# A two-layer cross-attention kernel: the transposed operands split by half of the tokens, the work between the layers and the last linear layer put in another order

## The chip, the cores and the metric

The kernel runs on one core of a Trainium2 chip. The metric is device time in microseconds (us); the time of the kernel before is the median of three runs. A profiled execution gives the trace that the prediction is worked out from.

## The reference, cut to what matters

1024 tokens (16 sequences of 64) of width 512 pass four residual blocks, all in fp32:

```
x += L0_attention(layernorm(x), ctx)   # 32 query heads, 8 key/value heads of 128, rope, tanh cap, masked softmax
x += L0_experts(layernorm(x))          # 4 low-rank experts of rank 16, the best 2 by router logits
x += L1_attention(layernorm(x), ctx)   # 16 query heads, 4 key/value heads of 96, keys from [ctx, x]
x += L1_linear(layernorm(x))           # x W^T + bias + 16 low-rank updates, merged into W
```

## The kernel before, in words

The tokens lie in eight tiles of 128 rows, `xt[0..7]`; tiles 0 to 3 are half 0, tiles 4 to 7 are half 1. The matmuls need tokens along the free dimension, so one tile `hT` (128 x 2 x 4 x 1024) holds the transposed context (index 0, loaded by DMA) and the transposed normalised x (index 1). `ln_stats` (L183) takes the statistics of a half on VectorE (DVE): `bn_stats` (L188) and `bn_aggr` (L189) per tile, then the square root on ScalarE (ACT, L191) and a reciprocal (L192). `normed[i]` is `ln_tile(i)` (L196): DVE scales the tile into `xn` (L199), TensorE (PE) makes four transposes into PSUM (`tp`, L202), ACT copies them into `hT` (L203). This happens four times for each tile: at the start, between the layers ahead of the experts and again ahead of layer 1's attention, and ahead of the last linear layer.

Buffers: PSUM has four tags of two buffers each. `pa` holds projections, `tp` and `mp`; `pb` holds scores, softmax sums and small transposes; `pc` holds the attention product; `pd` holds what is added into x. `xn` and the last layer's output `ot` share a tag of two buffers in SBUF.

The attention of a layer is cut into items. In layer 0 an item (kv, half, quad) has four steps: `l0_scores` (PE L317, tanh and exp on ACT, two masking passes on POOL, L331 and L334), `l0_norm` (PE sum L342, the DVE reciprocal `r` of 128x512, L344, POOL product L346), `l0_av` (PE L358, four ACT copies L367) and `l0_wo` (16 matmuls L379, DVE add into x L386). In layer 1 an item (kv, half, pair) has `l1_scores` (PE L577, DVE maximum L585, exp L590, POOL product L599), `l1_transpose` (L605), `l1_av` (L615, copies L623 and L627) and `l1_wo` (L635).

The order is written out by hand in slots. Each item takes 4 slots (`SLOTS`), its steps lie at fixed distances (`LAGS`), and `BETWEEN` slots separate the layers. Everything else (projections, norms, experts, linear layer) is a filler put into a slot. `_run` goes through the slots and emits a slot's steps first, then its fillers. PE takes its instructions in exactly this order (`manual_schedule` for PE alone); the orders of DVE, ACT and POOL are made by the tile framework. So PE waits wherever its next instruction is not ready.

h0 is the slot in which layer 0's last step on half 0 falls, 116; h1, for half 1, is 132; layer 1 begins at slot u0 = 136. The order around h0, half 0's change of layers (steps | fillers):

```
116 wo(7,0,1) scores(6,1,1) | q_chunk 3, ln_stats        122 av(6,1,1)               | experts gT + 4 outputs
117                         | normed 0, 1                123 norm(7,1,0)             | ln_stats
118 av(6,1,0)               | normed 2, 3                124 wo(6,1,1) scores(7,1,1) | normed 0, 1
119 norm(6,1,1)             | experts_mid                125                         | normed 2, 3
120 wo(6,1,0) scores(7,1,0) |                            126 av(7,1,0)               | v_chunk 0, 1 of layer 1
```

Half 1 follows at h1 in the same manner, spread among layer 1's projections and first items. `experts_mid` (L430) multiplies with the experts and the router (`mp`, L434), then a chain of some 18 small DVE operations with one exp on ACT makes the gated product `gm` (L475). `experts_out` (L483) transposes it (`gtp`, L487), copies it (`gT`, L489), and makes one output matmul per tile (`pm`, L494; even tiles use rows 0 to 63, odd ones rows 64 to 127), which DVE adds into x (L495).

At the end, `linear(i)` (L676) adds the bias to x on POOL (L677), multiplies `hT` with the merged weight (`pf`, 8 matmuls, L680), adds on DVE into `ot` (L688) and stores it from SyncE's queue (L689). Its order after the projections have run out, with the last items of layer 1 (unit (3,1), pairs p0 to p3):

```
258 linear 0 | 259 wo p0 | 260 av p1, scores p3 | 261 transpose p2 | 262 linear 1 | 263 wo p1
264 av p2, stats 4 5 | 265 transpose p3 | 266 normed 4, linear 2 | 267 wo p2, stats 6, normed 5
268 av p3 | 269 linear 3 | 270 normed 6 | 271 wo p3, stats 7, linear 4, 5, normed 7, linear 6, 7
```

Of the kernel before, what the change touches and what calls it, by code (L numbers as in the profile page):

```python
# [72 lines left out]
LAGS = ((0, 3, 6, 8), (0, 5, 8, 11))  # L73


BETWEEN = 8
AHEAD = 2


# [8 lines left out]
def two_layer_kernel(  # L88
# [33 lines left out]

    hT = const.tile([P, 2, KC, NTOK], F32, tag="hT", name="hT")
    xt = [const.tile([P, D], F32, tag=f"x{i}", name=f"x{i}") for i in range(NT)]
    cos_sb = const.tile([P, S], F32, tag="cos", name="cos_sb")
    sin_sb = const.tile([P, S], F32, tag="sin", name="sin_sb")
# [5 lines left out]
    def load_ctx(half):  # L134
        for c in range(KC):
            nc.sync.dma_start(
                out=hT[:, 0, c, ts(half, HALF)], in_=ctxT[ts(c, P), ts(half, HALF)]
            )

    def load_x(half):  # L140
# [55 lines left out]
    def ln_tile(i):  # L196
        mean, rstd = ln[i]
        xn = work.tile([P, D], F32, tag="xn", name="xn")
        nc.vector.tensor_scalar(xn, xt[i], mean, rstd, ALU.subtract, ALU.mult)  # L199
        tp = ps.tile([P, KC, P], F32, tag="pa", name="tp")  # L200
        for c in range(KC):
            nc.tensor.transpose(tp[:, c, :], xn[:, ts(c, P)], ident)  # L202
        nc.scalar.copy(hT[:, 1, :, ts(i, P)], tp)  # L203

    halves = [range(0, NT // 2), range(NT // 2, NT)]

# [33 lines left out]
    v0 = {}  # L240

    def l0_unit(kv, half):
        tok = ds(half * HALF, HALF)
        unit = {"kv": kv, "half": half}

        def rope(pr, dst):
            cos_b = cos_sb.unsqueeze(1).to_broadcast([P, HALF // S, S])
            sin_b = sin_sb.unsqueeze(1).to_broadcast([P, HALF // S, S])
            sh = work.tile([P, HALF], F32, tag="sh", name="sh")
            nc.scalar.copy(sh[0:64, :], pr[64:128, :])  # L250
            nc.scalar.copy(sh[64:128, :], pr[0:64, :])  # L251
            u = work.tile([P, HALF], F32, tag="u", name="u")
            nc.vector.tensor_tensor(  # L253
                u.rearrange("p (b t) -> p b t", t=S),
                pr.rearrange("p (b t) -> p b t", t=S),
                cos_b,
                ALU.mult,
            )
            w = work.tile([P, HALF], F32, tag="w", name="w")
            nc.gpsimd.tensor_tensor(  # L260
                w.rearrange("p (b t) -> p b t", t=S),
                sh.rearrange("p (b t) -> p b t", t=S),
                sin_b,
                ALU.mult,
            )
            nc.vector.tensor_tensor(dst, u, w, ALU.add)  # L266

        def k_chunk():
            unit["k"] = act.tile([P, HALF], F32, tag="k", name="kT")
            unit["q"] = act.tile([P, G0, HALF], F32, tag="q", name="qT")  # L270
            pr = ps.tile([P, HALF], F32, tag="pa", name="pk")
            for c in range(KC):
                nc.tensor.matmul(  # L273
                    pr, lhsT=w0[kv][1][:, c, :], rhs=hT[:, 0, c, tok], start=c == 0, stop=c == KC - 1
                )
            rope(pr, unit["k"])

        def q_chunk(g):
            pr = ps.tile([P, HALF], F32, tag="pa", name="pq")
            for c in range(KC):  # L280
                nc.tensor.matmul(  # L281
                    pr,
                    lhsT=w0[kv][0][:, c, ts(g, HD0)],
                    rhs=hT[:, 1, c, tok],
                    start=c == 0,
                    stop=c == KC - 1,
                )
            rope(pr, unit["q"][:, g, :])

        def v_chunk(n):  # L290
            if n == 0:
                v0[kv // 2] = act.tile([P, NT, 2 * HD0], F32, tag="v", name="v")
            pr = ps.tile([P, 2, 2 * HD0], F32, tag="pa", name="pv")
            for i in range(2):
                for c in range(KC):
                    nc.tensor.matmul(  # L296
                        pr[:, i, :],
                        lhsT=hT[:, 0, c, ts(2 * n + i, P)],
                        rhs=w0[kv][2][:, c, :],
                        start=c == 0,  # L300
                        stop=c == KC - 1,
                    )
            nc.scalar.copy(v0[kv // 2][:, 2 * n : 2 * n + 2, :], pr)

        context = [k_chunk]
        if half == 0 and kv % 2 == 0:
            context += [lambda n=n: v_chunk(n) for n in range(4)]
        queries = [lambda g=g: q_chunk(g) for g in range(G0)]
        return context, queries, [{"unit": unit, "quad": qd} for qd in range(2)]

# [119 lines left out]
    def experts_mid(grp):  # L430
        mp = ps.tile([P, 4, NM + NE], F32, tag="pa", name="mp")
        for n in range(4):
            for c in range(KC):
                nc.tensor.matmul(  # L434
                    mp[:, n, :],
                    lhsT=hT[:, 1, c, ts(grp * 4 + n, P)],
                    rhs=aw[:, c, :],
                    start=c == 0,
                    stop=c == KC - 1,
                )  # L440
# [39 lines left out]
        )  # L480
        experts[grp] = gm

    def experts_out(grp):  # L483
        gmf = experts[grp].rearrange("p n e r -> p (n e r)")
        tp = ps.tile([P, 2, P], F32, tag="pb", name="gtp")
        for m in range(2):
            nc.tensor.transpose(tp[:, m, :], gmf[:, ts(m, P)], ident)  # L487
        gT = work.tile([P, 2, P], F32, tag="gT", name="gT")
        nc.scalar.copy(gT, tp)  # L489
        for n in range(4):  # L490
            i = grp * 4 + n
            rows = slice((n % 2) * NM, (n % 2 + 1) * NM)
            po = ps.tile([P, D], F32, tag="pd", name="pm")
            nc.tensor.matmul(po, lhsT=gT[rows, n // 2, :], rhs=bcat[rows, :], start=True, stop=True)  # L494
            nc.vector.tensor_add(xt[i], po, xt[i])  # L495


# [4 lines left out]
    def l1_unit(kv, half):  # L502
# [1 line left out]
        nb = B // 2  # L504

        def k_chunk(n):
            tok = ds(half * HALF + n * 256, 256)
            pr = ps.tile([P, 2, 256], F32, tag="pa", name="pk1")
            for c in range(KC):
                nc.tensor.matmul(  # L510
                    pr,
                    lhsT=w1s[kv][1][:, c, :],
                    rhs=hT[:, :, c, tok],
                    start=c == 0,
                    stop=c == KC - 1,
                )
            prb = pr.rearrange("d s (b t) -> d b s t", t=S)
            nc.scalar.copy(unit["k"][:, n * 4 : n * 4 + 4], prb[0:HD1])
            b0 = half * nb + n * 4
            nc.scalar.copy(k_last[ts(kv, TH), b0 : b0 + 4], prb[HD1:P])  # L520
# [10 lines left out]
        def q_chunk(g):  # L531
            pr = ps.tile([P, HALF], F32, tag="pa", name="pq1")
            for c in range(KC):
                nc.tensor.matmul(  # L534
                    pr,
                    lhsT=w1s[kv][0][:, c, ts(g, P)],
                    rhs=hT[:, 1, c, ds(half * HALF, HALF)],
                    start=c == 0,
                    stop=c == KC - 1,
                )  # L540
# [4 lines left out]
        def v_chunk(b):  # L545
# [2 lines left out]
                v1[half] = act.tile([P, nb, KV1 * HD1], F32, tag="v", name="v1")  # L548
            hv = work.tile([P, KC, 2, S], F32, tag="sh", name="hv")
            for s in range(2):  # L550
                nc.gpsimd.tensor_copy(hv[:, :, s, :], hT[:, s, :, ts(b, S)])
            pr = ps.tile([P, KV1 * HD1], F32, tag="pa", name="pv1")
            for c in range(KC):
                nc.tensor.matmul(  # L554
# [121 lines left out]
    def linear(i):  # L676
        nc.gpsimd.tensor_tensor(xt[i], xt[i], bias_bc, ALU.add)  # L677
        po = ps.tile([P, D], F32, tag="pd", name="pf")
        for c in range(KC):
            nc.tensor.matmul(  # L680
                po,
                lhsT=hT[:, 1, c, ts(i, P)],
                rhs=lin["w"][:, c, :],
                start=c == 0,
                stop=c == KC - 1,
            )
# [85 lines left out]
    put(begin[0, (6, 1)] + 13, lambda: load_wo1(0))  # L772
    put(begin[0, (7, 1)] + 13, lambda: load_wo1(1))
    for half, t in ((0, h0), (1, h1)):
        at = (1, 3, 6, 7, 8) if half == 0 else (2, 4, 8, 9, 11)
        mine = [normed[i] for i in halves[half]]
        put(t, lambda half=half: ln_stats(*halves[half]))
        put(t + at[0], *mine[:2])
        put(t + at[0] + 1, *mine[2:])
        put(t + at[1], lambda half=half: experts_mid(half))  # L780
        put(t + at[2], lambda half=half: experts_out(half))
        put(t + at[3], lambda half=half: ln_stats(*halves[half]))
        put(t + at[4], *mine[:2])
        put(t + at[4] + 1, *mine[2:])
    spread(h0 + 10, u0 - 1, built1[0, 0][0])
    spread(u0 - AHEAD, begin[1, (1, 0)] - AHEAD, built1[1, 0][0])
    spread(h1 + 13, u1 - AHEAD, built1[0, 1][0])
    for a, b in zip(units1[2:], units1[3:]):
        spread(begin[1, a] - AHEAD, begin[1, b] - AHEAD, built1[b][0])
    for kv in (2, 3):  # L790
# [17 lines left out]
    def applied(i):  # L808
        return lambda: linear(i)

    put(last + 10, applied(0))
    put(last + 14, applied(1))
    put(last + 16, stats(4, 5))
    put(last + 18, normed[4], applied(2))
    put(last + 19, stats(6), normed[5])
    put(last + 21, applied(3))
    put(last + 22, normed[6])
    put(h1, stats(7), applied(4), applied(5), normed[7], applied(6), applied(7))
    _run(stages, fillers)


# [42 lines left out]
```

## Time and profile before

| | |
|---|---|
| median of three runs | 1091.32 us (1090.82 to 1091.77) |
| the profiled execution's own time | 1091.71 us |
| its span, first to last instruction | 1089.8 us |
| its mean granted PE clock | 0.994 |
| busy: PE, DVE, ACT, POOL | 96%, 40%, 30%, 27% of the span |
| DMA | 38.56 MB, mean 35 GB/s |

The table comes from the page's head and its first parts. A busy PE is counted with modelled ends of matmuls; the chain of waits shows how many microseconds a run of matmuls holds PE, and the windows show where it stood idle or had a lower clock.

### The profile page before, as it was taken

How to read it: one execution, taken by the hardware profiler on the slowest of the kernel's cores; microseconds unless marked ns; L12 is line 12 of the kernel's file. 1: busy time of each engine (PE TensorE's matmuls, PEld its weight loads, DVE VectorE, ACT ScalarE, POOL GpSimd, SP SyncE). 2: the span in 40 equal slices, each digit the busy share in tenths (PEclk: the TensorE clock that was granted, in tenths of full speed). 3: DMA queues.
4: the chain of work that ended last, by engine and by line, in shares of the span. 5: the costliest groups of instructions: out<-in, count | busy, mean ns of one | idle time of the engine just before them, and what ended most of it. 6: DMA issues, size and time to landing. Idle time of an engine off the chain costs nothing.

```text
span 1089.8 us, 9319 instructions
## 1 busy us (share of the span) xinstructions
PE 1051.7 (96%) x3398; PEld 532.3 (49%) x3398; DVE 436.3 (40%) x641; ACT 327.3 (30%) x844; POOL 291.8 (27%) x263
## 2 busy tenths in 40 slices
PE   7789999999999999999999999998999999999987
PEld 5334455444455444446444444545565555555643
DVE  3345342435432434432434555314322334435532
ACT  2342232232232232231322241224333343334420
POOL 2143332433331433331433331200121011112210
PEclk9999999999999999999999998999999999999999
DMA  9310020010020010020010100110001000110001
GB/s 320 102 39 0 11 78 19 10 53 25 11 78 14 10 46 31 11 78 15 1 38 10 39 30 0 29 29 1 1 22 39 18 30 29 29 39 1 1 29 49
DMA packets 26157, 38.56 MB, mean 35 GB/s; under 512 B 1824, under 2 KB 12064, under 8 KB 26112
## 3 DMA queue, kind: packets, MB, share of 16 engines
q1 hardware_dynamic: 25840, 37.63, 10.5%
q8 instruction: 27, 0.44, 0.2%
q0 software_dynamic: 272, 0.34, 0.2%
q14 instruction: 18, 0.15, 0.0%
HBM read 35.87 MB, written 2.10 MB: 35 GB/s over the span
## 4 chain that ended last, share of the span: by engine, by line
PE 93%; ACT 3%; DVE 2%; DMA 1%; POOL 1%; issue 0%; SPq 0%; DVEq 0%; ACTq 0%
PE pq L281 20%; PE po L379 20%; PE pq L534 8%; PE po L635 8%; PE pk L273 6%; PE pv L296 4%; PE pk L510 4%; PE pv L554 4%; PE sc L317 3%; PE av L358 3%; PE pf L680 3%; PE sm L342 3%; PE av L615 2%; PE sc L577 2%; PE tp L605 1%; PE tp L202 1%
## 5 line engine op out<-in xcount | busy, mean ns | idle before, releaser
L281 PE MATMUL pq<-hT,wq 128*128 128x512 f32 x512 | 234.3, 602 | 6.6 <-ACT hT L203 6.6
L379 PE MATMUL po<-wo,at 128*128 128x512 f32 x512 | 225.9, 594 | 0.0
L260 POOL TENSOR_TENSOR w<-sh,sin_sb 128x512 f32<-128x512 f32 x80 | 106.7, 1333 | 197.7 <-ACT sh L251 197.2
L379 PEld LDWEIGHTS po<-wo,at 128*128 128x128 f32 x512 | 97.8, 191 | 121.4 <-issue 120.2
L281 PEld LDWEIGHTS pq<-hT,wq 128*128 128x128 f32 x512 | 93.7, 190 | 123.2 <-issue 110.1
L344 DVE RECIPROCAL r<-sm 128x512 f32<-128x512 f32 x32 | 107.4, 3357 | 107.6 <-PE sm L342 107.6
L253 DVE TENSOR_TENSOR u<-pq,cos_sb 128x512 f32<-128x512 f32 x64 | 43.1, 673 | 142.7 <-ACT sh L251 142.7
L599 POOL TENSOR_TENSOR e<-e,sm 128x512 f32<-128x512 f32 x32 | 33.3, 1039 | 244.5 <-DVE sm L598 237.3
L635 PE MATMUL po<-wo_sb,at 128*128 128x512 f32 x192 | 87.8, 593 | 0.1
L250 ACT COPY sh<-pq 64x512 f32<-64x512 f32 x64 | 37.3, 582 | 166.9 <-PE pq L281 166.9
L534 PE MATMUL pq<-hT,wq_sb 128*128 128x512 f32 x192 | 86.5, 595 | 0.6 <-ACT hT L203 0.6
L331 POOL TENSOR_TENSOR e<-e,keep 128x512 f32<-128x512 f32 x32 | 40.5, 1266 | 170.0 <-ACT e L330 170.0
L386 DVE TENSOR_TENSOR x<-po,x 128x512 f32<-128x512 f32 x64 | 44.0, 687 | 99.9 <-PE po L379 99.9
L326 ACT ACTIVATE e<-sc 128x512 f32<-128x512 f32 x32 | 19.1, 597 | 204.4 <-PE sc L317 204.3
L273 PE MATMUL pk<-hT,wk 128*128 128x512 f32 x128 | 63.2, 637 | 5.2 <-DMA hT<-in_ctxT 5.0
L266 DVE TENSOR_TENSOR qT<-u,w 128x512 f32<-128x512 f32 x64 | 49.3, 771 | 31.8 <-POOL w L260 31.3
L346 POOL TENSOR_TENSOR en<-e,r 128x512 f32<-128x512 f32 x32 | 41.0, 1282 | 76.6 <-DVE r L344 76.6
L296 PE MATMUL pv<-wv,hT 128*128 128x256 f32 x256 | 57.6, 381 | 1.2 <-DMA wv<-in_wv 0.8
L635 PEld LDWEIGHTS po<-wo_sb,at 128*128 128x128 f32 x192 | 35.8, 190 | 41.3 <-issue 35.3
L534 PEld LDWEIGHTS pq<-hT,wq_sb 128*128 128x128 f32 x192 | 35.1, 190 | 39.7 <-issue 37.1
L296 PEld LDWEIGHTS pv<-wv,hT 128*128 128x128 f32 x256 | 48.3, 190 | 12.3 <-issue 4.0
L642 DVE TENSOR_TENSOR x<-po,x 128x512 f32<-128x512 f32 x32 | 22.1, 690 | 75.3 <-PE po L635 75.2
(111 smaller groups left out, 1130.1 us busy)
## 6 DMA issues: line engine op xcount, KB each, us to landing
wq<-in_wq SPq DMA_DIRECT2D x8, 1024.0 KB, 5.7
wo<-in_wo SPq DMA_DIRECT2D x8, 1024.0 KB, 5.1
wq_sb<-in_wq SPq DMA_DIRECT2D x4, 768.0 KB, 4.7
wo_sb<-in_wo SPq DMA_DIRECT2D x4, 768.0 KB, 4.6
wk<-in_wk SPq DMA_DIRECT2D x8, 256.0 KB, 2.7
hT<-in_ctxT SPq DMA_DIRECT2D x8, 256.0 KB, 5.5
wv<-in_wv SPq DMA_DIRECT2D x4, 512.0 KB, 5.4
x<-in_x SPq DMA_DIRECT2D x8, 256.0 KB, 7.2
```

Source lines behind the costliest of these rows:

```text
L260: nc.gpsimd.tensor_tensor(w.rearrange("p (b t) -> p b t", t=S), sh.rearrange("p (b t) -> p b t", t=S), sin_b, ALU.mult,)
L266: nc.vector.tensor_tensor(dst, u, w, ALU.add)
L273: nc.tensor.matmul(pr, lhsT=w0[kv][1][:, c, :], rhs=hT[:, 0, c, tok], start=c == 0, stop=c == KC - 1)
L281: nc.tensor.matmul(pr, lhsT=w0[kv][0][:, c, ts(g, HD0)], rhs=hT[:, 1, c, tok], start=c == 0, stop=c == KC - 1,)
L296: nc.tensor.matmul(pr[:, i, :], lhsT=hT[:, 0, c, ts(2 * n + i, P)], rhs=w0[kv][2][:, c, :], start=c == 0, stop=c == KC - 1,)
L344: nc.vector.reciprocal(r, sm)
L379: nc.tensor.matmul(po, lhsT=it["at"][:, g, ts(pr, P)], rhs=wo[:, g, :], start=g == 0, stop=g == G0 - 1,)
L386: nc.vector.tensor_add(xt[i], po, xt[i])
L510: nc.tensor.matmul(pr, lhsT=w1s[kv][1][:, c, :], rhs=hT[:, :, c, tok], start=c == 0, stop=c == KC - 1,)
L534: nc.tensor.matmul(pr, lhsT=w1s[kv][0][:, c, ts(g, P)], rhs=hT[:, 1, c, ds(half * HALF, HALF)], start=c == 0, stop=c == KC - 1,)
L554: nc.tensor.matmul(pr, lhsT=hv[:, c].rearrange("p s t -> p (s t)"), rhs=wv1s[c // 2][:, c % 2, :], start=c == 0, stop=c == KC - 1,)
L635: nc.tensor.matmul(po, lhsT=it["at"][:, g].rearrange("d m t -> d (m t)"), rhs=w1s[u["kv"]][2][:, g, :], start=g == 0, stop=g == PK1 - 1,)
```

## The change

`hT` becomes two tiles, one per half (`hT[h]`, 128 x 2 x 4 x 512), and each use names its half. `experts_out` is cut in two: `experts_gT` (transposes and copy) and `experts_out(grp, pair)` (two of the four outputs), in slots of their own. `BETWEEN` goes from 8 to 10, so layer 1 begins at slot 138. Between the layers and in the last linear layer the fillers get other slots:

```diff
-BETWEEN = 8
+BETWEEN = 10
...
-    hT = const.tile([P, 2, KC, NTOK], F32, tag="hT", name="hT")
+    hT = [const.tile([P, 2, KC, HALF], F32, tag=f"hT{h}", name=f"hT{h}") for h in range(2)]
...
-        nc.scalar.copy(hT[:, 1, :, ts(i, P)], tp)
+        nc.scalar.copy(hT[i // 4][:, 1, :, ts(i % 4, P)], tp)
...
-    def experts_out(grp):
+    def experts_gT(grp):
...
         nc.scalar.copy(gT, tp)
-        for n in range(4):
+        experts[grp] = gT
+
+    def experts_out(grp, pair):
+        for n in (2 * pair, 2 * pair + 1):
...
-        at = (1, 3, 6, 7, 8) if half == 0 else (2, 4, 8, 9, 11)
+        norm1, mid, gates, out0, norm2 = (2, 4, 7, 8, 11) if half == 0 else (3, 5, 9, 10, 14)
...
+        put(t + norm1, a, b)
+        put(t + norm1 + 1, c, d)
+        put(t + mid, lambda half=half: experts_mid(half))
+        put(t + gates, lambda half=half: experts_gT(half))
+        put(t + out0, lambda half=half: experts_out(half, 0))
+        put(t + out0 + 1, lambda half=half: experts_out(half, 1), lambda half=half: ln_stats(*halves[half]))
+        put(t + norm2, a, b)
+        put(t + norm2 + 1, c, d)
-    spread(h0 + 10, u0 - 1, built1[0, 0][0])
+    spread(h0 + 13, u0, built1[0, 0][0])
...
-    spread(h1 + 13, u1 - AHEAD, built1[0, 1][0])
+    spread(h1 + 16, u1 - AHEAD, built1[0, 1][0])
...
-    put(last + 10, applied(0))
-    put(last + 14, applied(1))
-    put(last + 16, stats(4, 5))
-    put(last + 18, normed[4], applied(2))
-    put(last + 19, stats(6), normed[5])
-    put(last + 21, applied(3))
-    put(last + 22, normed[6])
-    put(h1, stats(7), applied(4), applied(5), normed[7], applied(6), applied(7))
+    put(last + 15, stats(4, 5))
+    put(last + 18, applied(0))
+    put(last + 19, normed[4], stats(6))
+    put(last + 20, normed[5])
+    put(last + 22, applied(1))
+    put(h1, stats(7), applied(2), normed[6], applied(3), applied(4), applied(5))
+    put(h1 + 1, normed[7], applied(6), applied(7))
```

The same three places in the new order, worked out from the code. Around h0 (slot 116 unchanged but for what follows it):

```
117                         |                            123 norm(7,1,0)             | gT
118 av(6,1,0)               | normed 0, 1                124 wo(6,1,1) scores(7,1,1) | outputs 0, 1
119 norm(6,1,1)             | normed 2, 3                125                         | outputs 2, 3, ln_stats
120 wo(6,1,0) scores(7,1,0) | experts_mid                126 av(7,1,0)               |
121                         |                            127 norm(7,1,1)             | normed 0, 1
122 av(6,1,1)               |                            128 wo(7,1,0)               | normed 2, 3
```

Around h1: `normed 4, 5` follow layer 1's first k projection, `normed 6, 7` the first q projection; `experts_mid` and the last q projection stand directly ahead of layer 1's first `l1_scores` (138); gT comes at 141, outputs 4, 5 at 142, outputs 6, 7 and `ln_stats` at 143; then a q projection (145), av p0, scores p2, `normed 4, 5` (146), transpose p1, `normed 6, 7` (147). At the end: scores p3, transpose p2, wo p1, stats 4 5, av p2, transpose p3, linear 0, wo p2, normed 4, stats 6, av p3, normed 5, linear 1, wo p3, stats 7, linear 2, normed 6, linear 3, 4, 5, normed 7, linear 6, 7.

More of the change, by code (lines that the diff above doesn't have):

```diff
@@ L136, in load_ctx @@
             nc.sync.dma_start(
-                out=hT[:, 0, c, ts(half, HALF)], in_=ctxT[ts(c, P), ts(half, HALF)]
+                out=hT[half][:, 0, c, :], in_=ctxT[ts(c, P), ts(half, HALF)]
             )
@@ L242, in l0_unit @@
     def l0_unit(kv, half):
-        tok = ds(half * HALF, HALF)
         unit = {"kv": kv, "half": half}
@@ L273, in k_chunk @@
                 nc.tensor.matmul(
-                    pr, lhsT=w0[kv][1][:, c, :], rhs=hT[:, 0, c, tok], start=c == 0, stop=c == KC - 1
+                    pr, lhsT=w0[kv][1][:, c, :], rhs=hT[half][:, 0, c, :], start=c == 0, stop=c == KC - 1
                 )
@@ L283, in q_chunk @@
                     lhsT=w0[kv][0][:, c, ts(g, HD0)],
-                    rhs=hT[:, 1, c, tok],
+                    rhs=hT[half][:, 1, c, :],
                     start=c == 0,
@@ L297, in v_chunk @@
                         pr[:, i, :],
-                        lhsT=hT[:, 0, c, ts(2 * n + i, P)],
+                        lhsT=hT[n // 2][:, 0, c, ts(2 * (n % 2) + i, P)],
                         rhs=w0[kv][2][:, c, :],
@@ L435, in experts_mid @@
                     mp[:, n, :],
-                    lhsT=hT[:, 1, c, ts(grp * 4 + n, P)],
+                    lhsT=hT[grp][:, 1, c, ts(n, P)],
                     rhs=aw[:, c, :],
@@ L493, in experts_out @@
             po = ps.tile([P, D], F32, tag="pd", name="pm")
-            nc.tensor.matmul(po, lhsT=gT[rows, n // 2, :], rhs=bcat[rows, :], start=True, stop=True)
+            nc.tensor.matmul(
+                po, lhsT=experts[grp][rows, n // 2, :], rhs=bcat[rows, :], start=True, stop=True
+            )
             nc.vector.tensor_add(xt[i], po, xt[i])
@@ L506, in k_chunk @@
         def k_chunk(n):
-            tok = ds(half * HALF + n * 256, 256)
             pr = ps.tile([P, 2, 256], F32, tag="pa", name="pk1")
@@ L512, in k_chunk @@
                     lhsT=w1s[kv][1][:, c, :],
-                    rhs=hT[:, :, c, tok],
+                    rhs=hT[half][:, :, c, ds(n * 256, 256)],
                     start=c == 0,
@@ L536, in q_chunk @@
                     lhsT=w1s[kv][0][:, c, ts(g, P)],
-                    rhs=hT[:, 1, c, ds(half * HALF, HALF)],
+                    rhs=hT[half][:, 1, c, :],
                     start=c == 0,
@@ L550, in v_chunk @@
             for s in range(2):
-                nc.gpsimd.tensor_copy(hv[:, :, s, :], hT[:, s, :, ts(b, S)])
+                nc.gpsimd.tensor_copy(hv[:, :, s, :], hT[half][:, s, :, ts(b % nb, S)])
             pr = ps.tile([P, KV1 * HD1], F32, tag="pa", name="pv1")
@@ L681, in linear @@
                 po,
-                lhsT=hT[:, 1, c, ts(i, P)],
+                lhsT=hT[i // 4][:, 1, c, ts(i % 4, P)],
                 rhs=lin["w"][:, c, :],
@@ L774, in two_layer_kernel @@
     for half, t in ((0, h0), (1, h1)):
-        at = (1, 3, 6, 7, 8) if half == 0 else (2, 4, 8, 9, 11)
-        mine = [normed[i] for i in halves[half]]
+        norm1, mid, gates, out0, norm2 = (2, 4, 7, 8, 11) if half == 0 else (3, 5, 9, 10, 14)
+        a, b, c, d = [normed[i] for i in halves[half]]
         put(t, lambda half=half: ln_stats(*halves[half]))
[L778 to L784, printed above, removed]
-    spread(h0 + 10, u0 - 1, built1[0, 0][0])
+        put(t + norm1, a, b)
[7 more added lines that the diff above has]
+    spread(h0 + 13, u0, built1[0, 0][0])
     spread(u0 - AHEAD, begin[1, (1, 0)] - AHEAD, built1[1, 0][0])
-    spread(h1 + 13, u1 - AHEAD, built1[0, 1][0])
+    spread(h1 + 16, u1 - AHEAD, built1[0, 1][0])
     for a, b in zip(units1[2:], units1[3:]):
```

## The prediction, as put on record

> **What bounds the kernel now.** First the page's busy shares, then the windows, for the stretches in which PE is not full. Columns: stretch, its length, busy us of PE, PE loads, DVE, ACT, POOL, then the granted PE clock.
>
> ```profile
> PE 1051.7 (96%) x3398; PEld 532.3 (49%) x3398; DVE 436.3 (40%) x641; ACT 327.3 (30%) x844; POOL 291.8 (27%) x263
> ```
>
> ```profile
> 640.00:651.00 11.00, 9.04 (x44) 4.53 (x43) 6.76 (x11) 6.78 (x13) 4.80 (x5) 1.00 0.20 73
> 651.00:688.00 37.00, 33.19 (x130) 16.72 (x129) 20.47 (x39) 11.42 (x23) 8.29 (x8) 0.91 0.08 22
> 668.00:672.00 4.00, 4.00 (x5) 1.47 (x6) 3.15 (x6) 0.00 (x0) 0.00 (x0) 0.50 0.00 0
> 672.00:676.00 4.00, 4.00 (x7) 1.58 (x6) 2.69 (x2) 0.00 (x0) 0.00 (x0) 0.65 0.00 0
> 735.00:784.00 49.00, 43.70 (x177) 24.57 (x176) 20.21 (x53) 20.22 (x52) 4.76 (x7) 1.00 0.00 1
> 784.00:975.00 191.00, 191.00 (x677) 107.17 (x676) 65.93 (x134) 66.70 (x258) 26.46 (x31) 1.00 0.08 24
> 1048.00:1090.00 42.00, 31.30 (x85) 14.36 (x83) 11.92 (x25) 6.04 (x14) 5.08 (x4) 0.96 0.10 38
> ```
>
> PE is full in layer 1's middle (191 of 191) and stands idle in exactly the places that the change touches: half 0's change of layers (640 to 688), half 1's (735 to 784), the last linear layer (1048 on). The change adds no matmul, so it can only move PE's waits.
>
> To size them I take a stretch's wall time less the time that its PE work holds PE in the chain of waits: wo 6.87, a projection 3.44 to 3.63, mid 3.52, av 1.06, scores 1.01, norm 0.86, four transposes 0.44, v_chunk 2.58, layer 1's wo, av, scores 2.58, 0.86, 0.89; two expert outputs on different rows 1.13 together (L494).
> - Half 0, 634.0 to 687.3: 53.3, of it work 41.7; lost **11.6**, with 3.4 of it to the clock (half of 4.0, and 0.35 of 4.0).
> - Half 1, 687.3 to 783.2: 95.9, work 87.1; lost **8.8**.
> - End, 1047.3 to 1086.1: 38.7, work 29.7; lost **9.0** (1.7 by the clock, 0.96 in the last window).
>
> **The split of hT.** Would it take away waits? The waits list has "PE pq L281 <- ACT hT L203: 6.6, 5, 1.5", at the start, where half 0's queries alternate with half 1's transposes. The timeline says no:
>
> ```profile
> 39.54 0.59 ACT L203 COPY hT<-tp 128x512 f32<-128x512 f32 x1
> 39.55 0.69 DVE L253 TENSOR_TENSOR u<-pq,cos_sb 128x512 f32<-128x512 f32 x1 [0.28 <-ACT sh L251]
> 40.18 1.13 PE L281 MATMUL pq<-hT,wq 128*128 128x512 f32 x2 [1.50 <-ACT hT L203]
> ```
> ```profile
> 768.88 1.10 ACT L203 COPY hT<-tp 128x512 f32<-128x512 f32 x2 [1.45 <-PE tp L202]
> ```
>
> At 40.18 both `pa` buffers come free at once (the copy ends at 40.13, `u` at 40.24), so the query would wait for PSUM anyway. And a half-0 query at 769.52 started after the first of two half-1 copies, while the second ran until 769.98: no false dependence. I take 0; the bounds are 0 and the 6.6.
>
> **Half 0.** Waits in the new order, step by step.
> - First norm: av now stands ahead of transposes 0, whose `xn` is there at 646.17 (0.79 gone). Transposes 1 need PSUM, freed by an ACT copy behind the four av copies (1.2): 0.6 to 1.8, I take 1.1; transposes 3, 0.3. Sum 1.4.
> - norm(7,1,0) follows scores(7,1,0) by mid and av, 4.58. Its input needs tanh's table load (after a square root), tanh, exp, two POOL passes: 1.28+0.60+0.63+1.27+1.26 and hops, 5.35: wait 0.75. *ScalarE: Activation LUTs*, section *What ACT_TABLE_LOAD costs*, speaks against the change here: about 2.66 a switch, with a drain. That would make it 2.1. In the trace the load at 682.13 is followed by its tanh at 683.43, so I use 1.28.
> - gT is new in its place: only av and norm (1.92) stand between mid and it, where 8.9 stood. Half 1 shows the chain at 3.9 (752.94 to 756.85). With the 0.75: wait 0.9. If DVE puts `r` of norm(7,1,0), 3.36, into the chain while it waits for ACT's exp: 4.7. I take 0.9. Behind gT stand wo(6,1,1) and all of PE.
> - gT's copy is then under wo and scores (7.9), before 1.3 in the open. If that cover went, 1.3 is back. Outputs 2, 3 wait for `pd` behind DVE's adds (0.69 each): lost 1.5, as much as in half 1 before.
> - Second norm. From the end O of scores(7,1,1), outputs take until O+3.75, av and norm until O+5.7. Adds and statistics take 5.5 (half 1, 759.20 to 764.66): O+6.7. While ACT takes the square root DVE is free, and `r` of norm(7,1,1) is ready. Before, it already ran ahead of statistics that were ready:
>
> ```profile
> 671.41 0.69 DVE L495 TENSOR_TENSOR x<-pm,x 128x512 f32<-128x512 f32 x1
> 673.41 3.36 DVE L344 RECIPROCAL r<-sm 128x512 f32<-128x512 f32 x1 [1.31 <-PE sm L342]
> 676.68 0.12 DVE L189 BATCH_NORM_AGGREGATE mv<-st 128x2 f32<-128x6 f32 x1
> 676.73 1.25 DVE L188 BATCH_NORM_STATS2 st<-x 128x6 f32<-128x512 f32 x2
> ```
>
>  There wo (6.87) hid it; now nothing does. With `r` first, transposes 0 start at O+11.0: wait 5.3; without, O+8.0: 2.3. I take 5.3. wo(7,1,0) and layer 1's first v_chunks queue behind it.
> - Clock. *TensorE: Matmul & The Clock Gate*, section *HAM oscillation*, asks for PE gaps above some 3.4 before the clock halves. Here it fell to 0.50 at 668 after gaps of at most 1.5, so a stretch that is mostly idle is enough. By the page a gap of 2.3 costs nothing; by the row it may. For 5.3 both give one slow stretch, half of 3.4: 1.7 (0 to 3.4).
> - v_chunk 0 waits 0.3 for `pa`.
>
> Sum 1.4+0.75+0.9+1.5+5.3+1.7+0.3 = 11.85, against 11.6: **+0.25**. The stall moves, it does not go.
>
> **Half 1.** Transposes among projections wait for `pa` behind ACT copies: 1.8 (2.3 before). New: the last q projection stands directly ahead of the first scores, which need its two copies in turn (DVE 0.69, ACT 0.58, hops): 1.4. gT comes 9.2 after mid, against 3.9 needed, and the output pairs are 3.9 apart: 0. The second norm has 5.2 of PE work for 4.6 of chain: 0. Transposes 6, 7 and the query wait for ACT: before, av copies, a table load and four exps stood between two hT copies (775.53 and 778.81), so 0.6 to 2.9; I take 2.9, as that order is the one shown. 0.2 for hops. Sum 6.3: **-2.5**.
>
> **End.** normed 4 waited from 1048.5 to 1052.6 for add, statistics, root (4.0) and cost a slow stretch (1.7). Now 7.3 of PE work lies between (av, transpose, linear, wo), for a chain of 4.1: 0. Linear 0 and 1 no longer fill in: transpose p3 comes 3.9 after scores p3, whose chain took 4.65 (from 1013.0): 0.8. normed 5 is behind statistics 6 on DVE: 1.0 (0 to 1.35). normed 6 and 7 stay behind the `ot` emitted before them:
>
> ```profile
> 1065.80 0.69 DVE L688 TENSOR_TENSOR ot<-pf,x 128x512 f32<-128x512 f32 x1 [2.07 <-PE pf L680]
> 1066.41 0.54 DVE L199 TENSOR_SCALAR xn<-x,mv,rstd 128x512 f32<-128x512 f32 x1
> 1067.09 0.63 PE L202 MATMUL tp<-ident,xn 128*128 128x128 f32 x4 [1.40 <-DVE xn L199]
> ```
>
>  1.4 each, as now. Sum 4.6: **-4.4**. The moved linears bring a POOL add (1.27), a DVE add (0.69) and a store (landing in 2.0) each; POOL and SyncE's queue are empty there, so 0. Weight loads keep their distance to their units (landing in 4.7, tens of us ahead): 0. The two extra slots are emission order, not time.
>
> Sum: 0.25-2.5-4.4 = -6.65. On the profiled execution (1089.8 span and 1.9 around it, 1091.71) 1085.1; the median is 0.4 lower, so **1084.7**.
>
> **The rivals.** A measurement of this kernel tells about 0.2%, 2.2, from no change: 1089.1 to 1093.5 is the same.
> - A, the sum: 1084.7, own range 1081.5 to 1088. 0.38.
> - B, DVE takes the norm ahead of `r`: 3.0 and the clock's 1.7 less: 1080.0; if the split were worth its 6.6 after all, 1078.1. For it: the root is ready 0.4 after DVE gets free. 0.14.
> - C, the gate chain too is caught behind `r`: 3.8 and 1.7 of clock more: 1090.2. For it: before, an add waiting for PE stood between `sel` and the gates at 658.95. 0.21.
> - D, slower: the same 3.36 also ahead of `xn` 2 or 3 in the first norm, since norm(6,1,1) is now emitted ahead of them: 3.3 and 1.7 on top of C, 1095.2. It decides once half 0 loses 8.8 more than in A, which takes two of these places with their slow clock. Against it: `xn` 2 is ready about 1.5 sooner than `r`. 0.27, since one order serves all three places.
>
> **How the numbers follow.** Faster: A 0.36, B 0.14, C 0.05: 0.55. Same: 0.02 of A, 0.14 of C: 0.16. Slower: 0.27 and 0.02 of C: 0.29. The range reaches from B to D: 1079 to 1095.
>
> **What would show it.** `r` between the last statistics and `xn` in half 0's second norm, and PE idle for some 5 ahead of transposes 0, shows the main step; gT waiting under 1.5, C wrong. No wait at normed 4 and a clock of 1.00 in the last 40 us show the end. Queries at the start still waiting 1.5 show the split worthless. The prediction is wrong if DVE's order differs, or if layer 1's middle is no longer full.

## The result, and the profile after

The kernel after takes 1096.53 us (median of 7 runs, 1094.45 to 1099.06), the kernel before, run beside it, 1091.5 (7 runs, 1089.44 to 1093.59). The ratio is **1.0045, with a 95% interval of 1.0031 to 1.006**: slower by about half a per cent, where 1084.7, faster by 0.6%, was predicted. The profiled execution of after took 1094.45 with a span of 1092.7, the quickest of its runs; its mean PE clock was 0.991, before 0.994. Since one execution is traced of each kernel, what a trace shows can differ from a median by 2 to 3 us. The lines of after's code lie 1 to 4 further on than before's (`xn` L200, `tp` L203, `hT` L204, `gm` L475, `gtp` L487, `pm` L497, add into x L500, `ot` L692).

The work on PE is the same (busy 1051.1 us against 1051.7), so the page's first part says only that the waits and the clock changed:

```profile
PE 1051.1 (96%) x3398; PEld 532.5 (49%) x3398; DVE 435.8 (40%) x641; ACT 324.8 (30%) x842; POOL 292.6 (27%) x263
```

The windows, with the same columns as before (stretch, length, busy us of PE, PE loads, DVE, ACT, POOL, granted clock, DMA share, GB/s), say where. Half 0's change of layers, two pieces of it, half 1's, layer 1's middle, the end:

```profile
651.00:701.00 50.00, 38.91 (x140) 19.99 (x138) 24.54 (x45) 9.32 (x21) 9.86 (x9) 0.86 0.06 16
668.00:672.00 4.00, 3.81 (x6) 1.81 (x7) 0.04 (x1) 0.37 (x1) 1.17 (x1) 0.50 0.00 0
688.00:692.00 4.00, 1.53 (x7) 1.53 (x8) 3.21 (x5) 0.38 (x1) 1.26 (x1) 0.50 0.00 0
701.00:794.00 93.00, 86.62 (x295) 47.19 (x296) 26.42 (x65) 28.97 (x71) 10.04 (x21) 0.98 0.03 9
798.00:989.00 191.00, 190.89 (x676) 106.72 (x675) 68.29 (x140) 66.40 (x258) 26.75 (x30) 1.00 0.10 29
1050.00:1093.00 43.00, 36.11 (x100) 16.42 (x97) 12.33 (x25) 6.03 (x14) 5.07 (x4) 1.00 0.13 49
```

Layer 1's middle is still full and at the end PE is now busy 36.11 of 43 (before 31.30 of 42), at a clock of 1.00 in place of 0.96. Half 0 lost: 11 us idle out of 50, and two stretches at half the clock where before there was one.

In wall time, between the same instructions:

| stretch | before | after | change | predicted |
|---|---|---|---|---|
| start of the trace to wo(7,0,1) | 634.0 | 633.1 | -0.9 | 0 |
| half 0: wo(7,0,1) to v_chunk 0 | lost 11.6 | lost 18.7 | **+7.1** | +0.25 |
| half 1, to the v_chunk behind the last query | lost 8.8 | lost 10.3 | +1.5 | -2.5 |
| the end: linear 0 (after: wo p0, which now comes first) to the last `pf` | 52.9 | 48.1 | -4.8 | -4.4 |

"Lost" is the stretch less its PE work, as in the prediction. Half 0's stretch is 68.14 long after; 7.73 of that is work that lay behind it before (wo(7,1,0) and one sum), 41.7 is the old work. The sum, +2.9, is the difference of the spans; the -0.9 arose ahead of the first place whose order the change touches, where the first loads landed a little sooner (`pk` waited 4.4 for `hT<-in_ctxT`, before 5.0), and I do not count it as the change's.

What took half 0's time stands in two stretches of the timeline (columns: start, duration, engine, line, operation; idle time before it and its releaser in brackets). The first is the gate chain:

```profile
664.32 0.18 DVE L472 TENSOR_TENSOR gate<-gate,gs 128x16 f32<-128x16 f32 x1
664.41 3.35 DVE L344 RECIPROCAL r<-sm 128x512 f32<-128x512 f32 x1
667.68 0.36 DVE L475 TENSOR_TENSOR gm<-mid,gate 128x256 f32<-128x256 f32 x1
668.19 0.66 PE L487 MATMUL gtp<-ident,gm 128*128 128x128 f32 x2 [4.75 <-DVE gm L475]
```

The chain from `mid` to `gm` is done but for one operation of 0.36, when the reciprocal of norm(7,1,0) goes in between. PE, whose next instruction is `gtp`, waits 4.75.

In the kernel before, `gm` was long done when PE came to its transposes, which did not wait:

```profile
660.58 0.42 DVE L475 TENSOR_TENSOR gm<-mid,gate 128x256 f32<-128x256 f32 x1
664.35 0.44 PE L487 MATMUL gtp<-ident,gm 128*128 128x128 f32 x2
```

The second place is half 0's second norm:

```profile
685.40 3.33 DVE L344 RECIPROCAL r<-sm 128x512 f32<-128x512 f32 x1
686.28 0.30 ACT L192 ACTIVATE rstd<-mv,eps_c 128x4 f32<-128x4 f32 x1
688.64 0.12 DVE L193 RECIPROCAL rstd<-rstd 128x4 f32<-128x4 f32 x1
688.80 2.07 DVE L200 TENSOR_SCALAR xn<-x,mv,rstd 128x512 f32<-128x512 f32 x2
690.47 1.97 PE L203 MATMUL tp<-ident,xn 128*128 128x128 f32 x8 [5.27 <-DVE xn L200]
```

Here `r` of norm(7,1,1) runs while ACT takes the root. The root is done at 686.6, DVE comes to it at 688.64, and PE's transposes wait 5.27. Behind each of the two waits wo runs at half clock for a while: from its start to the start of what follows it takes 9.28 and 7.64 in place of 6.87.

At the start nothing has changed: the query at 39.32 waits 1.49 for the ACT copy into `hT`, as before.

At the end normed 4 and 5 follow without a wait; normed 6 (shown) and 7 still stand behind the `ot` ahead of them:

```profile
1067.79 0.69 DVE L692 TENSOR_TENSOR ot<-pf,x 128x512 f32<-128x512 f32 x1 [1.34 <-PE pf L684]
1068.40 0.54 DVE L200 TENSOR_SCALAR xn<-x,mv,rstd 128x512 f32<-128x512 f32 x1
1069.09 0.63 PE L203 MATMUL tp<-ident,xn 128*128 128x128 f32 x4 [1.40 <-DVE xn L200]
```

### The profile page after: what moved, and what is told of

It is laid out like the page before. It is cut to its first block, busy times and chain, and to the rows that moved or that the text cites. A ratio compares the mean times of both kernels' runs of the same rounds, so it can differ in the third digit from the quotient of the medians.

```text
span 1092.7 us, 9329 instructions
## 1 busy us (share of the span) xinstructions
PE 1051.1 (96%) x3398; PEld 532.5 (49%) x3398; DVE 435.8 (40%) x641; ACT 324.8 (30%) x842; POOL 292.6 (27%) x263
## 4 chain that ended last, share of the span: by engine, by line
PE 93%; DVE 3%; ACT 2%; DMA 1%; POOL 1%; issue 0%; SPq 0%; ACTq 0%; DVEq 0%
PE pq L281 21%; PE po L379 20%; PE pq L538 8%; PE po L639 8%; PE pk L273 5%; PE pv L296 5%; PE pv L558 4%; PE pk L514 4%; PE sc L317 3%; PE av L358 3%; PE pf L684 3%; PE sc L581 2%; PE sm L342 2%; PE av L619 2%; PE tp L609 1%; PE tp L203 1%
## 5 line engine op out<-in xcount | busy, mean ns | idle before, releaser
L386 DVE TENSOR_TENSOR x<-po,x 128x512 f32<-128x512 f32 x64 | 44.0, 687 | 107.2 <-PE po L379 107.2
L594 ACT ACTIVATE e<-sc,nmx 128x128 f32<-128x128 f32 x128 | 45.2, 365 | 21.5 <-DVE nmx L590 19.4
```

The costliest lines, as they stand in the source:

```text
L594: nc.scalar.activation(e[:, n, :], sc[:, n, :], AF.Exp, bias=nmx[:, n : n + 1], scale=SCALE1, accum_out=sm[:, n : n + 1],)
```

## The experiments

The theory drawn from these traces: the end gives its gain, the split gives nothing, and half 0 loses it all again, because `r` sits in both of its short chains (the gate's and the second norm's), where PE has too little work queued to hide 3.36 us. Rivals: that the later slots of half 0 themselves cost the time, `r` or not; that half 1's new order is what costs; that the split does something after all. The ratios below are against the kernel before, run beside each group of experiments (medians 1091.86, 1091.61 and 1091.92). "Less than after" compares a median with the 1096.53 above; the intervals of the two together leave such a difference uncertain by 2 to 3 us.

**The split alone.** The kernel before with `hT` in two tiles, all slots as they were (gT and its outputs in one slot).

> The kernel before with the split of hT alone; every slot as before. If the split is worth nothing, as predicted: 1091.5, within 0.2% of the kernel before, and the queries at the start still wait about 1.5 each for an hT copy. Rival, the split took away false waits: up to 6.6 less, 1085. Rival, the split is what made the change slow: 1096.

Measured: 1091.61 us, ratio 0.9996 (0.9986 to 1.0005). The waits list (total, times, longest) has the starting queries unchanged:

```profile
PE pq L281 <- ACT hT L204: 6.6, 5, 1.5
```

The split is worth nothing. With two tiles no query of half 0 depends on a copy into half 1's tile, and the waits are the same to 0.1 us; so what the query waits for can only be the PSUM buffer `pa` that the copy sets free, as the prediction read it from the timeline.

**The end alone.** The kernel before with the new slots of the last linear layer:

```diff
-    put(last + 10, applied(0))
-    put(last + 14, applied(1))
...
+    put(last + 18, applied(0))
+    put(last + 19, normed[4], stats(6))
...
```

> The kernel before with the last linear layer's new order alone. If the end's gain stands by itself: 52.9 from linear 0 to the last linear matmul becomes 48.1, so 4.8 less: 1086.7, and no wait of 4 at normed 4. Rival, the gain needs the two extra slots or the split: about 1091.5.

Measured: 1087.24 us, ratio 0.9957 (0.9944 to 0.997): 4.6 less than before. The waits for `xn` fall from 10.1 us, longest 4.0, to

```profile
PE tp L202 <- DVE xn L199: 6.1, 6, 1.6
```

which is the 4.0 of normed 4. So the end is a gain by itself, and the rest of the change costs it back and more: 1087.24 to 1096.53.

**Half 0 in its old slots, everything else new.**

```diff
+        if half == 0:
+            at = (1, 3, 6, 7, 8)
...
+            put(t + at[0], *mine[:2])
+            put(t + at[0] + 1, *mine[2:])
...
+        else:
             norm1, mid, gates, out0, norm2 = ...
```

> The changed kernel with half 0's fillers between the layers in their old slots (transposes, experts, outputs, second norm); half 1, end, split and the extra slots as changed. If half 0's new order costs the 7.1 that the traces differ there: 1096.5 - 7.1 = 1089.4, a little under the kernel before. Rival, the loss sits in half 1 or in layer 1's shift by two slots: 1095 or more.

Measured: 1088.84 us, ratio 0.9966 (0.9951 to 0.998), 7.7 less than the kernel after. The +7.1 that the traces show for half 0 is confirmed: the loss lies in the order of half 0's fillers.

**A short `r` in the two places.** For items (7, half 1) `r` is a copy of the sum (0.68 us) in place of its reciprocal; the softmax of these items is not divided, so the output isn't the reference's. Every slot is the kernel after's.

```diff
-        nc.vector.reciprocal(r, sm)
+        if (it["unit"]["kv"], it["unit"]["half"]) == (KV0 - 1, 1):
+            nc.vector.tensor_copy(r, sm)
+        else:
+            nc.vector.reciprocal(r, sm)
```

> The changed kernel, its order untouched, but the softmax reciprocal r of the two items (7, half 1) is a copy of the sums instead (the output is then not the reference's): about 0.65 on DVE in place of 3.36. If r in DVE's queue ahead of gm and of xn is the cause: gT's wait 4.75 becomes about 2.1, that of transposes 0 5.3 becomes about 2.6, and at least one of the two slow stretches of the clock goes: 6 to 9 less, 1088 to 1090.5. Rival, too little PE work in front of gT and of the transposes whatever DVE does: the waits stay above 4 and 4.5, 1095.

Measured: 1087.25 us, ratio 0.9952 (0.9935 to 0.9969), 9.3 less than after, a little more than the 6 to 9 expected. The gate chain in this kernel's timeline:

```profile
665.49 0.68 DVE L345 COPY r<-sm 128x512 f32<-128x512 f32 x1
666.65 0.41 PE L490 MATMUL gtp<-ident,gm 128*128 128x128 f32 x2 [2.15 <-DVE gm L478]
666.90 8.73 PE L382 MATMUL po<-wo,at 128*128 128x512 f32 x16
```

The copy stands exactly where the reciprocal stood; the wait falls by 2.6, from 4.75 to 2.15, and the second norm's from 5.27 to 2.60. These 5.3 us are the operation's length alone (2 x 2.7). In the traces half 0's stretch is 7.7 shorter than in after; the other 2.3 or so are clock: behind the second wait the transposes and wo now run at full speed (1.7 less), behind the first wo takes 8.66 in place of 9.28. The remaining 1.6 of the 9.3 is not located and lies within the intervals. The rival that `r` plays no part falls. That the slots leave too little PE work ahead stands beside `r`: 2.15 and 2.60 of wait are left without it.

**The order turned round.** The sums whose `r` does the harm are held back: norm(7,1,0) is emitted behind gT, norm(7,1,1) behind the first two tiles' transposes. Nothing is left out.

```diff
+                    if f is l0_norm and u == (KV0 - 1, 1):
+                        held.append(lambda it=it: l0_norm(it))
+                        continue
...
+    put(h0 + 7, held[0])
+    put(h0 + 11, held[1])
```

> The changed kernel with nothing left out, but the softmax sum of item (7,1,0) is emitted behind gT instead of ahead of it, and that of (7,1,1) behind transposes 0 and 1 of half 0's second norm; so neither reciprocal r can stand ahead of gm or of xn in DVE's order. PE work in front of gT and of the transposes gets even less (0.86 each). If r's place is the cause: gT waits about 2.6 (4.75 minus r, plus the 0.86), the transposes about 2.8 to 3.2 instead of 5.3, one slow stretch of the clock goes: 5 to 8 less, 1089 to 1091.5. Rival, too little PE work in front: the waits grow, 1097.

Measured: 1089.13 us, ratio 0.9975 (0.9962 to 0.9989), 7.4 less than after. From its timeline:

```profile
666.42 0.44 PE L487 MATMUL gtp<-ident,gm 128*128 128x128 f32 x2 [2.63 <-DVE gm L475]
684.02 1.11 PE L203 MATMUL tp<-ident,xn 128*128 128x128 f32 x8 [3.28 <-DVE xn L200]
686.36 8.19 PE L379 MATMUL po<-wo,at 128*128 128x512 f32 x16
```

Both waits are shorter although less PE work (no sum, 0.86) stands ahead of them. With the reciprocal still done, only later, this shows that the place of `r`, and not its work, costs these 7.4. The waits of 2.63 and 3.28 that are left are not its doing.

**More cover in place of less `r`** (the experiment e6_behind_wo). The kernel after, with gT behind wo(6,1,1) and the four transposes of half 0's second norm behind wo(7,1,0); `r` stays where it is.

```diff
-        put(t + gates, lambda half=half: experts_gT(half))
+        if half == 0:
+            stages[t + 8].insert(1, lambda: experts_gT(0))
...
-        put(t + norm2, a, b)
-        put(t + norm2 + 1, c, d)
+        if half == 0:
+            put(t + 12, a, b, c, d)
```

> The changed kernel, half 0 only: gT is emitted between wo(6,1,1) and scores(7,1,1), and all four transposes of the second norm stand behind wo(7,1,0). r stays ahead of gm and xn in DVE's order, but 6.87 of PE work covers it in both places. Both theories, r and too little cover, expect the waits at gT and at the transposes gone: of the 18.7 that half 0's stretch loses some 4.8 stay, 1082.8. If instead half 0's loss is the clock alone, or comes from elsewhere: 1092 or more.

Measured: 1081.49 us, ratio 0.9899 (0.9877 to 0.9921), 15.0 less than after. The timeline:

```profile
664.35 3.35 DVE L344 RECIPROCAL r<-sm 128x512 f32<-128x512 f32 x1
667.61 0.36 DVE L475 TENSOR_TENSOR gm<-mid,gate 128x256 f32<-128x256 f32 x1
670.48 0.38 PE L487 MATMUL gtp<-ident,gm 128*128 128x128 f32 x2
684.78 1.04 PE L203 MATMUL tp<-ident,xn 128*128 128x128 f32 x8
686.27 1.24 PE L203 MATMUL tp<-ident,xn 128*128 128x128 f32 x8 [0.46 <-DVE xn L200]
```

and the window of half 0:

```profile
640.00:700.00 60.00, 57.41 (x227) 30.39 (x226) 32.02 (x56) 20.86 (x43) 17.65 (x22) 1.00 0.08 27
```

`r` is still ahead of `gm`, at the same moment as in after; the gate's transposes and the norm's first two tiles do not wait, the last two tiles wait 0.46, the clock is 1.00, and PE is busy 57.4 of 60 (after: 48.15, before: 54.23). The traced execution is the quickest of the six, 1079.31; the other five have a mean clock of 0.997 or 0.998. Half 0's stretch is 13.5 shorter than in after, the two waits and their slow stretches. So half 0's new order is worth 7.4 against the old one with all else equal (1088.84), once wo lies in the right place. And of the 15.0 only 7.4 to 9.3 went when `r` was moved or shortened: the rest is the short cover itself, which lets PE wait even without `r`.

**The two covers apart.** One edit each, to see what each of the two waits is worth. First gT alone:

```diff
+        if half == 0:
+            stages[t + 8].insert(1, lambda: experts_gT(0))
```

> The kernel after with one edit: gT stands behind wo(6,1,1) in place of ahead of it, so that 6.87 of PE work covers the gate chain with r in it. The theory (r in the gate chain is the failed step: a wait of 4.75 and the slow stretch of 2.3 behind it) expects 7 less than the kernel after, less 0.3 for gT's copy, which only the scores hide now: 1089.8, and no wait ahead of the transposes of gm. The prediction's book (gT waits 0.9) expects 1095.6. If the two slow stretches hang together, so that the second stays or goes with the first, it is 1.8 less: 1088.

Measured: 1089.21 us, ratio 0.9975 (0.9965 to 0.9985): 7.3 less than after. The gate no longer waits; the second norm does as before, with its slow stretch, which is thus independent of the first:

```profile
684.30 1.97 PE L203 MATMUL tp<-ident,xn 128*128 128x128 f32 x8 [5.27 <-DVE xn L200]
```

Then the transposes alone:

```diff
+        if half == 0:
+            put(t + 12, a, b, c, d)
```

> The kernel after with the other edit alone: the four transposes of half 0's second norm behind wo(7,1,0). Takes away the wait of 5.27 and the slow stretch of 1.8 to 2.8 behind it: 1088.5 to 1089.5; gT still waits 4.75 with its slow stretch. If the two edits add up, the two gains together are the 15.0 that both brought in one kernel; if both waits are needed for the slow stretches, their sum is less than 15.

Measured: 1088.51 us, ratio 0.9965 (0.9949 to 0.9982): 8.0 less than after. The gate waits 4.8 and the windows behind it are slow:

```profile
668.00:672.00 4.00, 2.29 (x5) 1.29 (x6) 1.56 (x2) 0.37 (x1) 1.27 (x1) 0.62 0.00 0
672.00:676.00 4.00, 4.00 (x7) 1.60 (x6) 0.00 (x0) 0.00 (x0) 0.00 (x0) 0.53 0.00 0
```

7.3 and 8.0 make 15.3, against 15.0 for both in one kernel. That these agree to 0.3 is luck, given the intervals, but the traces say the same: half 0's stretch is 6.7 and 6.0 shorter, and 13.5 with both. So these are two separate losses of about the same size, each a wait of about 5 and a slow stretch of about 2.

**Half 1 in its old slots, everything else new.**

```diff
+        if half == 1:
+            at = (2, 4, 8, 9, 11)
...
+        else:
             norm1, mid, gates, out0, norm2 = ...
```

> The changed kernel with half 1's fillers between the layers in their old slots, all else as changed. From the traces, half 1's stretch lost 10.3 after and 8.8 before: 1.5 less than the changed kernel, 1095. As the prediction had it, half 1's new order is worth 2.5: 1099.

Measured: 1096.19 us, ratio 1.0042 (1.0031 to 1.0053), the same as after within the intervals. Of the two values named, its own interval rules out 1099 and just reaches 1095. Half 1's stretch takes 86.82 in this trace and 86.84 in after's. But after's holds a slow stretch of the clock (1.3) and this one does not; with the new slots and no slow stretch it takes 85.26 (e6_behind_wo). So half 1's new slots save 1.6 of waits against the old ones, and the clock took it back in six of the seven traces that have them. One new wait, of the first scores of layer 1 for the last query's copy, is there in this kernel too,

```profile
PE sc L581 <- ACT qT L547: 1.2, 1, 1.2
```

so it comes from spreading the first unit's projections up to u0, and not from half 1's slots. With the clock's 1.3 it is more than the +1.5 that the trace shows for half 1; the other waits are 1.0 shorter than before.

**All together.** The kernel with both covers, the spread ended one slot sooner, and half 1's last two transposes two slots later:

```diff
-    spread(h0 + 13, u0, built1[0, 0][0])
+    spread(h0 + 13, u0 - 1, built1[0, 0][0])
...
-            put(t + norm2 + 1, c, d)
+            put(t + norm2 + 3, c, d)
```

> e6_behind_wo and two moves for half 1: the last q projection of layer 1's first unit one slot earlier, so that the first projection of (1,0) and experts_mid stand between it and the first scores (its wait of 1.2 goes), and transposes 6 and 7 of the second norm two slots later, behind a q projection and an l1_wo, so that the exps and the table load that ACT runs first are hidden (2 to 3, and a slow stretch of the clock, 1.2). 3 to 5 less than e6: about 1079. If ACT's order there is only another wait in disguise: equal to e6.

Measured: **1077.9 us, ratio 0.9863 (0.984 to 0.9885)**: 1.4% faster than before, the fastest version here; each of its six executions is quicker than each of the kernel's with the covers alone. The scores' wait is gone from its waits list and the transposes wait for ACT half as long (4.0 in after):

```profile
PE tp L203 <- ACT hT L204: 1.9, 2, 1.3
```

These waits are 1.2 and 2.1 less, against 3.6 between the medians. The traced executions differ by only 1.1: from wo(7,0,1) on this one is 3.2 shorter, ahead of it 2.1 longer, where the first load landed later and a slow stretch near 77 us comes in. The last two edits were not tried one by one.

## Why the prediction was wrong, point by point

In the traces the prediction's sum is 9.6 off: 6.85 in half 0 and 4.0 in half 1, less 0.4 at the end and the 0.9 at the start. (The medians are 11.8 apart, 1096.53 against 1084.7, mostly because after's traced execution is 2.1 quicker than its median.) The largest single term is gT's wait.

- **What bounds the kernel**, and that only PE's waits can move: right. PE's work and layer 1's middle stayed as they were.
- **Split, 0**: right, and the reason too (1091.61 by itself).
- **End, -4.4**: right (-4.8 in the trace, -4.6 alone). normed 4 waits no more, 6 and 7 wait the 1.40 and 1.39 that the text foresaw; transpose p3 and normed 5 lose 0.5 and 0.1, where 0.8 and 1.0 were booked.
- **Half 0, first norm 1.4**: right (16.6 from wo(7,0,1) to the end of it, of that 15.2 work). `xn` 2 and 3 ran ahead of `r`, so the third place of rival D did not occur.
- **norm(7,1,0), wait 0.75**: did not occur (about 0); its probabilities were ready in time. The text put tanh's table load into their chain. The load was not in it: ACT ran it while PE was at the wo ahead, and tanh started as soon as the scores were there.

```profile
650.38 1.28 ACT L326 ACT_TABLE_LOAD   x1
657.64 0.60 ACT L326 ACTIVATE e<-sc 128x512 f32<-128x512 f32 x1 [5.97 <-PE sc L317]
```

So neither the 0.75 nor the 2.1, which came from the 2.66 for a table switch in *ScalarE: Activation LUTs* of the Trainium skill, section *What ACT_TABLE_LOAD costs*, was tried here. On that figure itself the trace sides with 1.28: the load at 684.98 took 1.28, and the root behind it started 0.02 after its end (686.28).
- **gT, "4.7 ... I take 0.9": this is the step that failed.** Measured 4.75, and 5.0 from the sum's place to `gtp`. The text had both ends and the mechanism of the high one, and chose the low one. That 4.75 lies so near 4.7 is luck in part: in the text a wait of 0.75 stood ahead of it, 5.45 in all, and that one did not come. It also took the wait for ACT's exp as the moment of danger, when DVE would stand idle. In the trace the exp had ended at 662.98 and was long used; `r`, whose sum was done by 663.4, went in at the very end of the chain, between the gate's last product (ended 664.50) and `gm`. The two ends were far apart, and two rows that the prediction had named spoke for 4.7: `r` at 673.41 ahead of statistics that were ready, and an add at 658.95 in the gate chain itself. It took the first over for the second norm and left the second to rival C.
- **Second norm 5.3**: right (5.27), with `r` where it was expected.
- **Clock 1.7: too small.** It was booked for one wait. With two waits there were two slow stretches, each about 2 (wo 2.4 longer behind the first; transposes and wo 0.9 and 0.8 behind the second: 4.1). The end's slow stretch went, as foreseen; half 1 has a short new one (one query took 4.72 in place of 3.44). The stretch ahead of 668 in before, from which the text took that "mostly idle" is enough, was about half idle: PE was busy 1.94 of the 4 us from 664.
- **Outputs 1.5, v_chunk 0.3**: 1.8 and 0.5.
- **Half 1, -2.5: wrong in size**, in all about as large a miss as gT: the trace shows +1.5. Its terms: transposes among projections 2.2 (1.8 taken), first scores 1.4 (1.4), outputs behind gT's copy 0.7 (0), transposes 6, 7 and the query 3.7 (2.9), the clock 1.3 (0); they make 9.3 of the 10.3, and the last 1.0 is in gaps of about 0.1. Each of the misses is small, and all but the first scores went the same way.

Half 0's sum was 6.85 too small: gT 4.1, the clock 2.4, and 1.1 in small pieces, less 0.75 for norm(7,1,0); the small pieces are outputs 0.3, second norm 0.2, v_chunk 0.2, `mp` and `gtp` 0.4. Rival C had the mechanism (its 1090.2 took it on top of a half 1 that gained). Rival D named 1095.2 and the time came out near it, but that is luck: its third place did not happen, and what it adds there is in truth half 1's missing 2.5 and a bit more clock. The point that D set, 8.8 more lost in half 0 than in A, was not reached (6.85).

What stays open: what decides that DVE takes `r` ahead of `gm`. The traces show it in every kernel that has half 0's new slots, with `r` whole or short and with gT ahead of wo or behind it, and not in the kernel in which the sum is emitted behind gT; the rule by which the order is made was not examined. What decides whether a wait is followed by a slow clock stays open too (last section).

## What to carry to other kernels

If one engine runs in a fixed order and the others are ordered by a framework, look for the longest instruction of the other engines whose input is ready anywhere in a short dependent chain, and assume that it goes in: here one reciprocal of 3.36 us, in two such chains, cost 7 to 9 us of the 15 that the two waits and their slow stretches cost. Count the cover of a chain in microseconds of PE work between its start and its consumer, and not in slots; two slots that hold only a sum and a product hid 1.9, which is too short for the chain even without the reciprocal, while one `wo` hid 6.87 and made the place of the reciprocal irrelevant. And where a row of the trace decides an unknown cost in one place, use it for the other places of the same kind, or say why not.

## What the runs showed that was not expected

- A wait can cost more than its length, through the clock, but the length of the idle gap alone does not say whether. Gaps of 4.75 and 5.27 were each followed by a stretch at 0.50 (in the windows of 4 us above), which agrees with *TensorE: Matmul & The Clock Gate* of the Trainium skill, section *HAM oscillation*, where gaps above some 3.4 are what re-throttles. But with the short `r` a gap of 2.15 was followed by a slow wo (8.66 in place of 6.87), and in the same run a gap of 2.60 was not (6.87); with the sums held back, 2.63 was not (6.96) and 3.28 was (8.03).
- Nor does the place decide. Near 77 us, where every kernel has the same order, PE waits 2.08 or 2.09 for POOL's `en` in all twelve traces. In nine of them the projection behind it takes 4.6 to 5.2, in three (the end alone, the short `r`, both covers) 3.54. First after, then the kernel with both covers:

```profile
75.57 1.74 PE L358 MATMUL av<-en,v 64*128 64x256 f32 x8 [2.08 <-POOL en L346]
77.24 4.74 PE L273 MATMUL pk<-hT,wk 128*128 128x512 f32 x8
```
```profile
77.14 1.13 PE L358 MATMUL av<-en,v 64*128 64x256 f32 x8 [2.08 <-POOL en L346]
78.20 3.70 PE L273 MATMUL pk<-hT,wk 128*128 128x512 f32 x8
```

So executions differ in this, those of one kernel too: the 22 of the order turned round have mean clocks from 0.991 (1094.06 us) to 0.998 (1084.93 us). A slow stretch of 1 to 2 us behind a gap of 2 to 3 in a single trace is therefore not yet a property of the kernel, and no run here settles what decides it.
- Taking out 2.7 us of DVE work twice brought 9.3, and moving 6.87 of PE work twice brought 15: both above the bare waits removed (5.3 and 10.0). In the traces 2.3 and 4.1 of the difference are clock; the rest is not located.
